# Gates made in the first stage, both orders summed token-major, strands by arrival

## The chip, the cores and the metric

The kernel runs on one core of a Trainium2 chip. Its engines have their own queues: TensorE (PE, matmuls; PEld is its weight load), VectorE (DVE), ScalarE (ACT), GpSimd (POOL), and SyncE (SP), which here issues all transfers. The metric is the device time of one execution, the median of several runs, in microseconds.

## The reference

Four layers follow each other on an image batch of 8 x 256 x 32 x 32: an attention with a gated feed-forward, a second attention with an MLP, a quantized bottleneck, and a selective scan (Mamba) over four orders of the pixels. The change lies in the last layer. Cut to what matters:

```python
xs = concat([rows, rows reversed, columns, columns reversed])   # each (b, L, 256), L = 1024
def _mamba(u, ...):
    x, z = split(u @ W_in.T, 2)                 # 512 channels each
    x = silu(causal_conv4(x) + conv_b)
    x_dbl = x @ W_x.T                           # dt (16), B (16), C (16)
    dt = softplus(x_dbl[:16] @ W_dt.T + b_dt)
    h = h * exp(dt * A) + dt * B * x            # 16 states per channel, in order of the tokens
    y = einsum(h, C) + x * D
    return (y * silu(z)) @ W_out.T
out = y1 + flip(y2) + transpose(y3) + transpose(flip(y4))
```

z depends on the pixel alone, so the four orders share one gate: the kernel sums y of the four orders first and multiplies the sum by silu(z) once.

## The kernel before

**Two stages.** `phase_a` does the first three layers for each sample, and then the sample's `mix`: the x half of the last layer's input projection, the causal convolution in both directions along rows (k = 0) and columns (k = 1), and silu, all stored to DRAM (`mixes`). The output of layer 2 is stored too, as bf16 `codes`. `phase_b` does the scans. It has 64 blocks: sample, then order (`swap` 0 rows, 1 columns), direction (`back`), and half of 512 tokens. A block has 16 steps, one for each state; a step has four scans (DVE), one for each 128 channels. So a sample has eight blocks.

**How the order of the work is made.** Each task is a generator, a strand. It yields an operation, a list of them, or a condition. `_Order.run` (L313) takes, among the strands whose next operation is ready, the one that could start first by a table of costs (L108 to L143), and among equal starts the one with the lowest `(rank, number)`, the number being the order in which strands were added. What it picks is emitted, so every engine's queue is in a fixed order before the kernel runs. `_Room`s are sets of buffers that strands take and put back. In both stages `keep_dense` (L276) adds filler matmuls on a constant tile (`minus`) where PE would stand idle for long.

**First stage.** `sample(b)` (L1141) has rank (2, b); its parts have ranks (0, b), (1, b), (3, b), `mix(b)` rank (2, b). So at equal starts an earlier sample goes first, its convolutions too. `mix` (L1164) runs for one sample at a time. For each of four channel chunks it projects 2 x 512 tokens (six bf16 matmuls each), copies the result from PSUM on DVE (L1205), makes four convolution branches of four DVE operations each over 1024 tokens, reorders rows to columns by a POOL copy (L1210), and ends each pair of branches with a batch of silu on ACT and a table load (L1184).

**Second stage.** For a step: ACT scales rows of dt\*x (`dbu`), PE transposes them to `db`; ACT makes `da` = exp(dt\*A); DVE scans; POOL multiplies the states by C (`h<-h,cb`); PE sums the products over the 16 steps into four banks `py`, token-major, by transposes that accumulate (`sums`, L1643). At the end of a block `moved` (L1676) takes py to the tile `yT`. The two directions of an order meet there: the second block of a forward pass and the first of a backward pass share py, the other two meet in yT by an addition. One PSUM bank, `pp`, is lent (L1338) to all side work: dt, the transposes of dt\*x, and what follows.

**Sums and gates before.** After the second and third block of every order, `fold` (L1459) transposes yT back to channels, four chunks for the half at hand, and copies it to the tiles `ys` (row order) or adds it to them through a transposed view (column order). `outputs(b, h)` (L1483) runs for half h of the sample before, in blocks 0 and 2 of the next sample: it loads the codes and z's weights, projects z (`project`, L1344), scales it on DVE, waits for a batch of silu that `tables` (L1436) joins with a softplus batch, multiplies ys by it on POOL (L1497), and makes two output products (`o3`, four matmuls of 512 columns each), which ACT copies and SP stores. For the last sample both halves come after the last scan.

Of the kernel before, what the change touches and what calls it, by code (L numbers as in the profile page):

```python
# [29 lines left out]
P = 128  # L30
# [46 lines left out]
def tile_conv_seq(ctx: ExitStack, tc: tile.TileContext, i: dict, out: bass.AP):  # L77
# [19 lines left out]
    ]  # L97

    parts = [dram.tile([P, CC, 3, P], BF16, name=f"w_in{m}", tag=f"w_in{m}") for m in range(2 * DC)]

    phase_a(tc, i, col, ident, codes, parts, mixes)
    phase_b(tc, i, col, ident, codes, parts, mixes, out)
# [242 lines left out]
def phase_a(ctx, tc, i, col, ident, codes, w_parts, mixes):  # L345
# [29 lines left out]
    RANK = lambda b: (2, b)  # L375
# [386 lines left out]
    def layer0(b, x):  # L762
        rank = b
# [103 lines left out]
    def feed_forward(b, x):  # L867


        rank = b  # L870
# [112 lines left out]
    def layer1(b, x):  # L983
        rank = b
# [179 lines left out]
    def mix(b):  # L1164


        def branch(c, k, src, back, left):
            o = yield from take(mx)

            def span(t, j):  # L1170
                return (t[:, : N - j], src[:, j:]) if back else (t[:, j:], src[:, : N - j])

            yield V.tensor_scalar(o, src, col("cv_w", 4 * c + PAD), col("cv_b", c), ALU.mult, ALU.add)
            for tap in range(PAD):
                to, x = span(o, PAD - tap)
                yield V.scalar_tensor_tensor(to, x, col("cv_w", 4 * c + tap), to, ALU.mult, ALU.add)
            left[back] = o

        def both(c, k, src):
            left = {}  # L1180
            for back in (False, True):
                order.add(RANK(b), branch(c, k, src, back, left))
            yield lambda: len(left) == 2
            ops = [A.activation(o, o, AF.Silu) for o in left.values()]  # L1184
            yield (2.58 + sum(o.cost for o in ops), ops + [_Table()])
            for back, o in left.items():
                yield S.dma_start(mixes[b][k][back][c], o)
                put(mx, o)

        def chunk(c):  # L1190
# [5 lines left out]
            for h in range(2):  # L1196
# [3 lines left out]
                yield [  # L1200
                    T.matmul(ps, lhsT=w[:, k, e], rhs=xc[:, k], start=(k == e == 0), stop=(k == CC - 1 and e == 2))
                    for k in range(CC) for e in range(3)
                ]
                put(low, xc)
                yield V.tensor_scalar(xi[:, hs(h)], ps, col("s3"), None, ALU.mult)  # L1205
# [4 lines left out]
            yield G.tensor_copy(xp.rearrange("p (b a) -> p b a", a=HH), xi.rearrange("p (a b) -> p b a", b=WW))  # L1210
# [32 lines left out]
    with tc.manual_schedule():  # L1243
        for b in range(B):
            order.add((2, b), sample(b))
        order.add((9, B), weight_parts())
        order.run()
# [14 lines left out]
def phase_b(ctx, tc, i, col, ident, codes, w_parts, mixes, out):  # L1262
# [23 lines left out]
    z_room = _Room(rooms, "z", DC, [P, HALF])  # L1286
    wi_room = _Room(rooms, "wi", 2, [P, CC, 3, P], BF16)
    xf_room = _Room(rooms, "xf", 1, [P, CC, HALF], BF16)
# [33 lines left out]
    yT = wp.tile([P, NT, DI], F32, name="yT", tag="yT")  # L1322
    ys = [wp.tile([P, N], F32, name=f"ys{c}", tag=f"ys{c}") for c in range(DC)]
# [5 lines left out]

    def load_x(b, h, box):  # L1330

        xf = yield from take(xf_room)
        yield S.dma_start(xf, codes[b][:, :, hs(h)].rearrange("k p n -> p k n"))
        box.append(xf)
# [8 lines left out]

    def project(box, m0):  # L1344


        yield lambda: bool(box)
        w = yield from take(wi_room)
        yield S.dma_start(w, w_parts[m0 // P])
        room, ps = yield from lend()  # L1350
        yield [
            T.matmul(ps, lhsT=w[:, k, e], rhs=box[0][:, k], start=(k == e == 0), stop=(k == CC - 1 and e == 2))
            for k in range(CC) for e in range(3)
        ]
        put(wi_room, w)
        box.append(None)
        if len(box) == DC + 1:
            put(xf_room, box[0])
        return room, ps
# [74 lines left out]
    gates = {(b, h): {} for b in range(B) for h in range(2)}  # L1434

    def tables(m=None, z=None):  # L1436

        def ready():
            return (m is None or len(raw[m]) == DC) and (z is None or len(gates[z]) == DC)

        yield ready
        ops = []
        if z is not None:
            ops += [A.activation(t, t, AF.Silu) for t in gates[z].values()]
        if m is not None:
            ops += [A.activation(t, t, AF.Softplus) for t in raw[m].values()]
        loads = 1 + (z is not None) + (m is not None)
        yield (1.28 * loads + sum(o.cost for o in ops), ops + [_Table()])
        if m is not None:
            blocks[m][0].done[blocks[m][1]].add("soft")  # L1450
        if z is not None:
            gates[z]["done"] = True

    clear = {0: True, 1: True}
    folds = {b: [0, 0] for b in range(-1, B)}
    given = {b: 0 for b in range(-1, B)}
    given[-1] = 2 * CC

    def fold(b, swap, h):  # L1459

        left = [DC]

        def one(c):
            yield lambda: (folds[b][0] == 2 * DC if swap else given[b - 1] == 2 * CC)
            room, ps = yield from lend()
            yield [
                T.transpose(ps[:, t * P : (t + 1) * P], yT[:, h * TH + t, c * P : (c + 1) * P], ident)
                for t in range(TH)
            ]
            left[0] -= 1  # L1470
            if not left[0]:
                clear[h] = True
            if swap:
                y = ys[c].rearrange("p (a b) -> p b a", b=WW)[:, 16 * h : 16 * h + 16]
                yield V.tensor_tensor(y, ps.rearrange("p (a b) -> p a b", b=WW), y, ALU.add)
            else:
                yield V.tensor_copy(ys[c][:, hs(h)], ps)
            put(room, ps)
            folds[b][swap] += 1

        return [one(c) for c in range(DC)]

    def outputs(b, h):  # L1483
        box, done = [], set()

        def first():
            yield from load_x(b, h, box)

        def gate(c):
            t = yield from take(z_room)  # L1490
            room, ps = yield from project(box, DI + c * P)
            yield V.tensor_scalar(t, ps, col("s3"), None, ALU.mult)
            put(room, ps)
            gates[b, h][c] = t
            yield lambda: "done" in gates[b, h] and folds[b][1] == 2 * DC
            y = ys[c][:, hs(h)]
            yield G.tensor_tensor(y, y, t, ALU.mult)  # L1497
            done.add(c)
            put(z_room, t)

        def o3(cc):
            yield lambda: len(done) == DC
            o = yield from take(z_room)
            room, ps = yield from lend()
            for c in range(DC):
                yield T.matmul(
                    ps, lhsT=w_o3[:, c, cc * P : (cc + 1) * P], rhs=ys[c][:, hs(h)],
                    start=(c == 0), stop=(c == DC - 1),
                )
            yield A.copy(o, ps)  # L1510
# [3 lines left out]
            given[b] += 1  # L1514
# [161 lines left out]
    def moved(n, d, h, py):  # L1676

        if n % 4 != 3:
            yield lambda: clear[h]
            clear[h] = False  # L1680
        for t in range(TH):
            o = yT[:, h * TH + t, :]
            if n % 4 == 3:
# [5 lines left out]
            put(py_room, py[t])  # L1689
        if n == len(blocks) - 1:  # L1690
            spare.append(py_room)
        if n % 4 > 1:
# [158 lines left out]
```

## Time and profile before

| what | us |
|---|---|
| median of 3 runs (9354.29 to 9357.71) | 9355.51 |
| the profiled execution's own time | 9359.27 |
| its span in the profile | 9357.5 |
| first scan | 3807.0 |
| end of the last scan | 9324.4 |

Busy time of the engines by stage, from windows of the trace:

| stage | length | PE | DVE | ACT | POOL |
|---|---|---|---|---|---|
| first | 3807.0 | 3540 | 3006 | 2676 | 370 |
| second | 5517.4 | 5154 | 5221 | 5314 | 5292 |
| tail | 33.1 | 27 | 9 | 6 | 13 |

PE's busy time holds the fillers (1994 of them in the first stage). Busy time in a row of the profile is the union over the row's instructions, and the mean is that of one from start to end; where instructions overlap, busy divided by count is shorter than the mean. Nearly all operations are issued from one line of a helper (L154), so groups are told apart by the names of their tiles.

### The profile page before, as it was taken

What the parts mean: (1) busy time and instruction counts of PE and PEld (TensorE: products, weight loads), DVE (VectorE), ACT (ScalarE), POOL (GpSimd) and SP (SyncE); (2) the same over time, 40 slices, a digit from 0 to 9 for tenths busy, and PEclk for the clock granted to TensorE, in tenths of its full rate; (3) what the DMA queues carried; (4) which work ended last, traced back from release to release, by engine and by line L of the source; (5) the groups of instructions that cost most, each with busy time, mean ns of one, the idle gap of its engine ahead of it and who ended that gap; (6) DMA issues with size and microseconds to landing.
All of it is one profiled execution on the core that took longest, in us unless ns stands there. A gap on an engine that the chain in (4) does not pass through costs nothing.

```text
span 9357.5 us, 152821 instructions
## 1 busy us (share of the span) xinstructions
PE 8721.1 (93%) x56752; PEld 5778.5 (62%) x56752; DVE 8236.6 (88%) x9134; ACT 7996.2 (85%) x15039; POOL 5674.9 (61%) x2742
## 2 busy tenths in 40 slices
PE   9999999999999998799999999999999999999998
PEld 3333333333333333688788788778788788787787
DVE  7688587969899777899999999999999999999898
ACT  7768576767777774899999999999999999999998
POOL 0010010101111100799999999999999999999999
PEclk9999999999999999999999999999999999999999
DMA  1100111111111112222222212212222222222221
GB/s 57 38 25 22 38 55 49 48 35 49 34 64 57 39 52 85 76 64 66 69 65 66 73 61 65 73 61 67 71 62 68 69 67 65 68 67 64 69 66 58
DMA packets 297420, 548.41 MB, mean 59 GB/s; under 512 B 31761, under 2 KB 98705, under 8 KB 291554
## 3 DMA queue, kind: packets, MB, share of 16 engines
q1 hardware_dynamic: 296674, 538.64, 17.8%
q8 instruction: 446, 7.31, 0.3%
q14 instruction: 300, 2.46, 0.1%
HBM read 427.90 MB, written 100.14 MB: 56 GB/s over the span
## 4 chain that ended last, share of the span: by engine, by line
ACT 24%; PE 24%; DVE 16%; issue 3%; POOL 1%; DMA 0%; DVEq 0%; SPq 0%; POOLq 0%; ACTq 0%
ACT da L154 11%; DVE h L154 11%; ACT dbu L154 9%; PE db L154 8%; PE py L154 7%; PE pp L154 5%; PE bank L154 3%; DVE mx L154 1%; DVE mid L154 1%; DVE stats L154 1%; DVE ys L154 1%; ACT dt L154 1%; ACT L154 1%; DVE yT L154 1%; ACT st L154 1%
## 5 line engine op out<-in xcount | busy, mean ns | idle before, releaser
L154 POOL TENSOR_TENSOR h<-h,cb 128x1024 f32<-128x1024 f32 x2048 | 4798.5, 2388 | 144.2 <-ACT st L154 79.8
L154 ACT ACTIVATE da<-dt,am 128x512 f32<-128x512 f32 x4096 | 2867.8, 714 | 138.5 <-DVE h L154 130.7
L154 DVE TENSOR_TENSOR_SCAN h<-da,db 128x512 f32<-128x512 f32 x2048 | 2330.3, 1199 | 227.9 <-PE db L154 132.2
L154 DVE TENSOR_TENSOR_SCAN h<-da,st,db 128x512 f32<-128x512 f32 x2048 | 2444.0, 1258 | 68.1 <-PE db L154 47.3
L154 ACT ACTIVATE dbu<-du,bT 128x512 f32<-128x512 f32 x3584 | 2476.9, 708 | 9.3 <-PE db L154 5.0
L154 PE MATMUL db<-ident,dbu 128*128 128x128 f32 x14336 | 2134.6, 277 | 316.0 <-DVE h L154 303.6
L154 PE MATMUL py<-ident,h 128*128 128x128 f32 x16384 | 2121.5, 273 | 10.4 <-POOL h L154 6.5
L154 PEld LDWEIGHTS db<-ident,dbu 128*128 128x128 f32 x14336 | 1614.4, 141 | 748.0 <-DVE h L154 486.2
L154 PEld LDWEIGHTS py<-ident,h 128*128 128x128 f32 x16384 | 1849.9, 140 | 29.9 <-POOL h L154 10.6
L154 ACT ACTIVATE bank<-bank,stats 128x512 f32<-128x512 f32 x1536 | 1018.8, 676 | 369.8 <-DVE stats L154 362.8
L154 DVE TENSOR_REDUCE stats<-bank 128x1 f32<-128x512 f32 x1536 | 976.4, 680 | 222.0 <-PE bank L154 218.0
L154 ACT ACTIVATE exps<-bank 128x512 f32<-128x512 f32 x1536 | 793.8, 612 | 194.7 <-PE bank L154 189.6
L154 PE MATMUL bank<-big,big 32*128 32x512 f32 x4096 | 873.8, 659 | 40.7 <-ACT bank L154 18.2
L154 DVE SCALAR_TENSOR_TENSOR mid<-mid,cols,mid 128x961 f32<-128x961 f32 (+2 forms) x560 | 726.0, 1296 | 12.5
L154 POOL COPY mx<-mx 128x1024 f32<-128x1024 f32 x28 | 64.4, 2301 | 903.6 <-DMA mix<-mx 534.9
L154 PEld LDWEIGHTS bank<-big,big 32*128 32x128 f32 x4096 | 297.5, 190 | 480.0 <-issue 209.9
L302 PE MATMUL bank<-minus 128*128 128x512 bf16 x1994 | 522.5, 404 | 37.7 <-ACT exps L154 17.5
L154 PE MATMUL db<-dg,du 128*128 128x128 f32 x4096 | 530.4, 279 | 17.0 <-DVE h L154 16.1
L154 PE MATMUL bank<-exps,big 128*32 128x512 f32 (+1 forms) x3072 | 538.7, 611 | 0.0
L154 POOL TENSOR_TENSOR mid<-mid,mid 128x512 f32<-128x512 f32 x64 | 102.6, 1623 | 689.8 <-DVE mid L154 630.4
L154 PEld LDWEIGHTS db<-dg,du 128*128 128x128 f32 x4096 | 488.7, 192 | 49.3 <-DVE h L154 26.3
L302 PEld LDWEIGHTS <-minus 128*128 128x128 bf16 x2080 | 197.4, 102 | 491.9 <-issue 294.3
(204 smaller groups left out, 9271.5 us busy)
## 6 DMA issues: line engine op xcount, KB each, us to landing
cb<-c_d SPq DMA_DIRECT2D x1024, 256.0 KB, 3.2
xs<-mix SPq DMA_DIRECT2D x256, 256.0 KB, 4.3
mix<-mx SPq DMA_DIRECT2D x112, 512.0 KB, 3.0
big<-in_x_dram SPq DMA_DIRECT2D x16, 1024.0 KB, 5.3
kept<-big SPq DMA_DIRECT2D x16, 1024.0 KB, 5.2
big<-kept SPq DMA_DIRECT2D x16, 1024.0 KB, 6.9
low<-codes SPq DMA_DIRECT2D x64, 256.0 KB, 3.7
wi<-w_in SPq DMA_DIRECT2D x64, 192.0 KB, 3.4
```

Of the source, the lines that this page charges most:

```text
L154: return getattr(getattr(nc, self.engine), self.method)(*self.args, **self.kw)
L302: self.nc.tensor.matmul(x, lhsT=self.minus, rhs=rhs, start=True, stop=True)
```

## The change

The gates move: `mix` projects z for 512 tokens beside each pair of branches, applies silu straight from PSUM in the same batch as the branches' silu, and stores it to a new DRAM tensor `gates`. `phase_b` only loads it, into ten buffers instead of four. In `mix` the copy of xi from PSUM and the reordering copy go from DVE and POOL to ACT.

The sums change: `yT` becomes two tiles, one for each order, and `fold` and `ys` go. For each chunk and half, `gate` gathers both orders in one bank: four transposes of the row order's tile, and on top eight matmuls with the column order's tile as weights and 64 columns of the identity as moving data, taken through a permuted view, written to four of every 32 positions. DVE multiplies the bank by the loaded gate. A gate waits until all sums of the sample are in (`full`). `outputs` runs in blocks 0 and 1 of the next sample instead of 0 and 2.

All ranks of the first stage lose the sample's number: equal starts go to the strand that was added first. The samples' own strands are added at the beginning, `mix` later.

```diff
-    RANK = lambda b: (2, b)
+    RANK = lambda b: (2, 0)
...
     def layer0(b, x):
-        rank = b
+        rank = 0
...
         def both(c, k, src):
             left = {}
...
+            yield lambda: left and DC + c in made
+            w, xc = yield from projected(DC + c, k)
             yield lambda: len(left) == 2
+            ps = yield from side()
+            yield project(ps, w, xc)
+            put(low, xc)
+            put(low, w)
+            z = yield from take(low)
             ops = [A.activation(o, o, AF.Silu) for o in left.values()]
+            ops.append(A.activation(z, ps, AF.Silu, scale=col("s3")))
             yield (2.58 + sum(o.cost for o in ops), ops + [_Table()])
-            for back, o in left.items():
-                yield S.dma_start(mixes[b][k][back][c], o)
+            back(ps)
+            yield S.dma_start(gates[b][c, :, hs(k)], z)
+            put(low, z)
+            for way, o in left.items():
+                yield S.dma_start(mixes[b][k][way][c], o)
                 put(mx, o)
...
-                yield V.tensor_scalar(xi[:, hs(h)], ps, col("s3"), None, ALU.mult)
+                yield A.activation(xi[:, hs(h)], ps, AF.Identity, scale=col("s3"))
...
-            yield G.tensor_copy(xp.rearrange("p (b a) -> p b a", a=HH), xi.rearrange("p (a b) -> p b a", b=WW))
+            yield A.copy(xp.rearrange("p (b a) -> p b a", a=HH), xi.rearrange("p (a b) -> p b a", b=WW))
...
         for b in range(B):
-            order.add((2, b), sample(b))
+            order.add((2, 0), sample(b))
...
-    z_room = _Room(rooms, "z", DC, [P, HALF])
-    wi_room = _Room(rooms, "wi", 2, [P, CC, 3, P], BF16)
-    xf_room = _Room(rooms, "xf", 1, [P, CC, HALF], BF16)
+    z_room = _Room(rooms, "z", 10, [P, HALF])
...
-    yT = wp.tile([P, NT, DI], F32, name="yT", tag="yT")
-    ys = [wp.tile([P, N], F32, name=f"ys{c}", tag=f"ys{c}") for c in range(DC)]
+    yT = [wp.tile([P, NT, DI], F32, name=f"yT{k}", tag=f"yT{k}") for k in range(2)]
...
-    def fold(b, swap, h):
...
+    turned = ident.rearrange("p (b a) -> p a b", b=4)
...
         def gate(c):
-            t = yield from take(z_room)
-            room, ps = yield from project(box, DI + c * P)
-            yield V.tensor_scalar(t, ps, col("s3"), None, ALU.mult)
-            put(room, ps)
-            gates[b, h][c] = t
-            yield lambda: "done" in gates[b, h] and folds[b][1] == 2 * DC
-            y = ys[c][:, hs(h)]
-            yield G.tensor_tensor(y, y, t, ALU.mult)
-            done.add(c)
-            put(z_room, t)
+            yield lambda: c in zz and full[b] == FULL
+            room, ps = yield from lend()
+            yield [
+                T.matmul(
+                    ps[:, t * P : (t + 1) * P], lhsT=yT[0][:, h * TH + t, c * P : (c + 1) * P], rhs=ident,
+                    is_transpose=True, start=(t == 0), stop=False, skip_group_check=True,
+                )
+                for t in range(TH)
+            ] + [
+                T.matmul(
+                    ps.rearrange("p (a b) -> p a b", b=WW)[:, :, 4 * t : 4 * t + 4],
+                    lhsT=yT[1][:, t, c * P : (c + 1) * P], rhs=turned[:, 16 * h : 16 * h + 16],
+                    start=False, stop=(t == NT - 1), skip_group_check=True,
+                )
+                for t in range(NT)
+            ]
...
+            yield V.tensor_tensor(zz[c], ps, zz[c], ALU.mult)
             put(room, ps)
+            left[1] -= 1
...
-            z = (d.b - 1, n % 8 // 2) if n > 4 and n % 8 in (0, 2) else None
+            z = (d.b - 1, n % 8) if n > 4 and n % 8 in (0, 1) else None
...
-                jobs.append((SOFT, tables(m, z)))
+                jobs.append((SOFT, tables(m)))
             if z is not None:
-                jobs += zip((0, 1, 3, 4, 5, 12, 13), outputs(*z))
+                jobs += zip((0, 1, 3, 5, 7, 9, 11), outputs(*z))
```

## The prediction

> **What bounds the kernel now.** I read the whole page first (busy shares and the forty slices), then windows cut at stage borders, then windows of one sample of the second stage block by block, then the rows of the operations that the change touches.
>
> The page's first two parts:
>
> ```profile
> span 9357.5 us, 152821 instructions
> PE 8721.1 (93%) x56752; PEld 5778.5 (62%) x56752; DVE 8236.6 (88%) x9134; ACT 7996.2 (85%) x15039; POOL 5674.9 (61%) x2742
> DVE  7688587969899777899999999999999999999898
> POOL 0010010101111100799999999999999999999999
> ```
>
> There are two regimes. Until the sixteenth slice GpSimd is idle; then four engines are full at once. The first scan starts at 3807 us and the last ends at 9324, so the first stage is 3807 us, the second 5517, the tail 33. The profiled execution took 9359.27 us, 1.8 over its span; the median of the runs is 9355.51, so 3.8 come off a sum made against the profile.
>
> The first stage in windows between the moments at which sample 2, 5 and 7 finish layer 2 (the stores of their codes), and to the stage's end; columns are PE, PE weight loads, DVE, ACT and POOL busy, then granted clock and DMA:
>
> ```profile
> 2051.00:3225.00 1174.00, 1103.35 (x5206) 416.64 (x5205) 1065.40 (x1414) 863.36 (x1840) 138.85 (x82) 0.95 0.14 49
> 3225.00:3674.00 449.00, 420.08 (x2150) 149.21 (x2147) 319.45 (x466) 303.75 (x598) 34.93 (x24) 0.95 0.17 62
> 3674.00:3774.00 100.00, 54.59 (x238) 23.68 (x236) 85.61 (x73) 35.79 (x31) 9.50 (x4) 0.80 0.30 111
> ```
>
> In the middle DVE is 91% busy: it is the bound there. Later it is 71%, and chains set the pace. The last 100 us are the convolutions of sample 7 alone, on DVE.
>
> The second stage, sample 3, cut at every 64th scan (one block of sixteen steps):
>
> ```profile
> 5862.00:5959.00 97.00, 90.35 (x661) 73.94 (x660) 85.11 (x85) 87.36 (x164) 85.79 (x42) 0.98 0.22 67
> 5959.20:6043.60 84.40, 78.60 (x623) 68.27 (x622) 81.35 (x76) 81.16 (x131) 82.94 (x40) 1.00 0.22 67
> 6043.60:6133.50 89.90, 86.30 (x644) 71.62 (x643) 79.50 (x79) 87.51 (x166) 84.66 (x42) 1.00 0.24 74
> 6133.50:6219.70 86.20, 81.12 (x650) 71.21 (x649) 84.38 (x81) 82.56 (x133) 84.39 (x40) 1.00 0.21 64
> 6219.70:6303.40 83.70, 77.92 (x616) 67.41 (x615) 81.00 (x82) 80.85 (x155) 76.63 (x37) 1.00 0.19 60
> 6303.40:6386.10 82.70, 76.36 (x611) 66.89 (x610) 80.72 (x75) 81.92 (x133) 82.70 (x39) 1.00 0.22 67
> 6386.10:6467.20 81.10, 76.40 (x610) 66.83 (x608) 76.28 (x74) 80.95 (x157) 81.10 (x39) 1.00 0.21 66
> 6467.20:6555.00 87.80, 81.27 (x641) 70.22 (x641) 86.04 (x81) 83.94 (x135) 85.27 (x41) 1.00 0.22 68
> ```
>
> Blocks 5 and 6 hold nothing but scans and their preparation: POOL is busy for all of 82.7 and 81.1 us. That is the floor. Blocks 0 and 2 carry a half of the gates and outputs of the sample before (+14.3 and +8.8 over it), blocks 0, 3, 4, 7 a fold (four groups of transposes, four additions or copies). The eight take 692.8 us where eight at the floor take some 655.
>
> The rows that price the change:
>
> ```profile
> L154 PE MATMUL pp<-ident,yT 128*128 128x128 f32 x496 | 85.5, 284 | 15.3 <-DVE ys L154 10.5 <-DVE yT L154 4.6
> L154 PE MATMUL py<-dd,xs 128*128 128x128 f32 x2048 | 268.9, 275 | 0.0
> L154 PEld LDWEIGHTS db<-dg,du 128*128 128x128 f32 x4096 | 488.7, 192 | 49.3 <-DVE h L154 26.3
> L154 PE MATMUL bank<-low,low 128*128 128x512 bf16 x384 | 98.1, 396 | 14.1 <-DMA low<-codes 12.0 <-DVE mx L154 1.0 <-ACT bank L154 0.6
> L154 ACT ACTIVATE big<-bank,temp 128x512 f32<-128x512 f32 x32 | 22.1, 694 | 36.9 <-PE bank L154 36.9
> L154 DVE TENSOR_SCALAR mx<-bank,cols 128x512 f32<-128x512 f32 x56 | 41.7, 745 | 67.3 <-PE bank L154 67.0
> ```
>
> Busy divided by count is the spacing: 0.131 us for a pass of an fp32 matmul over 128 columns (each such matmul is two passes: 2048 records for 1024 matmuls), 0.119 for its weight load.
>
> **Second stage, blocks without outputs.** All folds go, and the outputs move from blocks 0 and 2 to blocks 0 and 1 (the instruction order of the changed kernel has the gates at steps 2 to 7 and the two output products at steps 9 to 11 of both). What stays is the same block without its extras. Block 2 falls from 89.9 to the 81.6 that it took in the first sample, where it has no outputs (-8.3); block 3 from 86.2 to 82.7, like block 5 (-3.5); block 4 from 83.7 to 82.5 (-1.2); block 7 from 87.8 to 82.7 (-5.1). Sum -18.1 a sample. POOL holds them there: 32 products at 2.34 us (4798.5/2048), 5.1 for four tmp, 2.1 for two dg, 82.1 in all.
>
> **Blocks 0 and 1.** Four gate items now cost no ACT (four silu, one table load: 2.2 + 1.3), no POOL (5.0 of ys times z) and one DVE multiplication each of about 0.68 (the yT addition's row, same operands) in place of 0.74 and of the folds' 1.15. What is left is PE: four transposes at 0.156 (2.5/16 in block 3) and sixteen passes over 64 columns with a full weight load. No row has that shape. From above 0.131, the 128-column pass; from below 0.065, half of it (512 columns take 0.513, so columns count). I take 0.119, since the weight load isn't shortened. A gate is 0.62 + 1.90 = 2.53 us, four are 10.1, the output products 7.2 (their row in block 0). On a base of 76.4 (blocks 5, 6) that is 93.7 us of PE in a block, above POOL's 82: **PE becomes the bound of these two blocks.** With 3 us of gaps each (block 2 has 3.6) they need 193.4. But PE can put off the py transposes: in block 0 today they start up to 17 us after their product, elsewhere 4 to 5, and nine h buffers allow it. I give back 10: 183.4 against 181.4 now, +2. Ends: all hidden, 2 x 82.7, -16; or 0.131, nothing put off, gaps of 6.65 as in block 0, 202.3, +21. The waits "DVE h <- ACT da" 3.8 and "DVE h <- PE db" 5.0 in block 0 and their like in block 2 go with the silu batch, which held ACT for 8.9 us at a stretch; 5.1 remain (softplus).
>
> The Trainium skill, TensorE: Matmul & The Clock Gate, sections "Back-to-back issue gap" and "LDWEIGHTS (loading the stationary operand)", speaks against the halved columns: spacing comes from weight load and matmul together, and the load goes by its 128 columns, P/1.2. As an estimate 107 ns a pass; the two blocks would be 181.9 and the forecast some 12 us lower.
>
> Seven samples carry outputs: 7 x (-18.1 + 2) = -113, ends -239 and +20. The first sample gains in blocks 3, 4, 7 (85.1, 84.3, 87.8 to 82.7, 82.5, 82.7): -9. **Second stage -122 (-248 to +11).** The new wait, a gate for the last yT sum, has the next db transposes behind it on PE and the scans behind those; today's yT transposes wait for the same additions (4.6 us in their row, over the whole run).
>
> **Tail.** Now 26.0 us from the first yT transpose (9331.5) to the end: 8.4 until the output products, 13.9 of these, 3.7 for copy and store. The gates of both halves wait for the last sum, so PE runs 8 x 2.53 = 20.2 first, then the same. **+12** (0.065 to 0.131: +5 to +13).
>
> **First stage.** Added on ACT: 64 evictions of xi and 64 silu from PSUM at 0.69, 32 copies at 1.05 (the row of that size): 122 us. Off DVE: 56 x 0.745 + 8 x 0.744 = 48. Off POOL 74. PE gains 384 bf16 matmuls at 0.256 = 98 and has 387 filler matmuls of 0.262 fewer (101). SP issues 192 more transfers here and 16 fewer loads later (0.3 to 0.5 us each on a queue with 2000 in 9 ms). Behind the gate's store on SP stand the two stores of mix, which wait for the same silu batch anyway; behind the gates' loads in the second stage stand the cb loads, and the gates' ten buffers are free when they issue, so I price SP at nothing; a cb late by its 3.2 us of landing would show as POOL idle. The gate's projection takes two low buffers and one bank for some 6 us, so maxima, limited to three banks beside an attention, may wait; that is in the ends below.
>
> Ranks are equal now, so ties fall to the strand added first, and the convolutions of an early sample no longer go ahead of a later sample's layers. Pricing every DVE instruction of both orders by the mean of its row shows it: between the codes of samples 2 and 5 the work falls from 1070 us to 949, between 5 and 7 it grows from 319 to 371, after 7 from 82 to 120. ACT, priced alike: 840 to 805, then 298 to 369. Before sample 2 DVE is even, ACT +33.
>
> - Up to sample 2: no engine is bound (DVE 75%). 0 (-20 to +35, all added ACT on the path).
> - 2 to 5: at 91% DVE, 949 us are 1046, -128; some stalls aren't DVE's, so -100 (-128 to 0).
> - 5 to 7: chains; put-off work falls into DVE's 130 idle us. +15 (0 to +71).
> - After 7: 120 at the 86% of now is 140, +40 (+20 to +60).
>
> **First stage -45 (-128 to +166).** What hides the added ACT work is its 30% of idle time; if that cover goes, up to 122 show.
>
> **Sum.** 9357.5 - 45 - 122 + 12 = 9202.5, as a median about 9200.
>
> **Rivals.**
> 1. *ACT is the first stage's chain* (ends slower). For it: the last long chain of the page has 24% ACT, and "ACT bank <- DVE stats" makes both one chain. Against: ACT is 74% busy in the middle, DVE 91%. Price: all 122, nothing from DVE, and the late convolutions +40: +162, giving 9405. It decides once the first stage loses over 129.
> 2. *PE eats the second stage's gain*: the upper end above, +11 and +13: 9357.5 - 45 + 24, as a median 9333. For it: PE is 93% busy in block 0. Against: py has been put off before.
> 3. *All at POOL's floor*: -248 and +9: 9070. For it: POOL is full in blocks 5 and 6 with PE at 92%. Against: 17 us more of PE per block.
>
> **How the numbers follow.** Forecast 0.65, rivals 0.11, 0.13, 0.11. No change means within 0.2% (19 us), about what a measurement here can tell. Rival 2 lies at that border: half of it is the same. Slower is rival 1 and a little of both stages failing. Faster 0.81, same 0.06, slower 0.13. The likeliest alone is 9110 to 9290; to hold 8 in 10 the range goes to rivals 3 and 2: 9070 to 9340.
>
> **What would show it.** Second stage: blocks 2, 3, 4, 7 at 81 to 83 us with POOL full; blocks 0 and 1 at 88 to 95 with PE over 95% busy; spacing of the 64-column passes 0.10 to 0.13; no POOL rows of ys. First stage: its end near 3760, sample 5's codes some 100 us earlier, the DVE-only end near 140 us. It is wrong if blocks 0 and 1 pass 100 us, or if sample 5's codes come no earlier than 3225.

## The result and the profile after

The changed kernel takes 9284.88 us (median of four runs, 9275.05 to 9289.06), against 9356.61 of the kernel before on the same chip: a ratio of 0.9915 with a 95% interval of 0.9903 to 0.9927, so 68 to 91 us less, where some 155 were forecast. The profiled execution has a span of 9287.3 us. Its first scan starts at 3807.2 (3807.0 before), its last scan ends at 9239.3, and the tail is 48.1. So **all of the gain lies in the second stage (-85), the tail gives 15 back, and the first stage gains nothing.**

From the first two parts of its page:

```profile
span 9287.3 us, 153572 instructions
PE 8701.5 (94%) x57003; PEld 5821.0 (63%) x57097; DVE 8034.5 (87%) x8940; ACT 8059.9 (87%) x15119; POOL 5517.7 (59%) x2648
DVE  7688677787987976899999999999999999899998
POOL 0010010000001000699999999999899899899998
```

DVE has 202 us less to do and POOL 157 less, ACT 64 more. GpSimd has no row of `ys` left.

The first stage in windows between the stores of the codes of samples 2, 5 and 7, and to its last convolution; columns are PE, PE weight loads, DVE, ACT and POOL busy, then granted clock, DMA and GB/s:

```profile
2021.00:3123.00 1102.00, 1044.91 (x4870) 388.64 (x4903) 924.33 (x1268) 831.40 (x1742) 93.04 (x62) 0.95 0.18 61
3123.00:3645.00 522.00, 485.72 (x2420) 177.31 (x2441) 365.85 (x526) 377.96 (x729) 31.81 (x24) 0.95 0.21 72
3645.00:3774.00 129.00, 90.38 (x373) 37.99 (x377) 117.25 (x103) 87.24 (x83) 0.00 (x0) 0.92 0.60 204
```

Sample 2's codes are 30 us earlier than before, the stretch to sample 5 is 72 shorter, that to sample 7 is 73 longer, and the end 29 longer: it sums to nothing. In the long stretch DVE is only 70% busy and ACT 72%.

Sample 3 of the second stage, cut at every 64th scan, with the same columns:

```profile
5836.70:5928.40 91.70, 90.27 (x713) 79.68 (x712) 82.07 (x82) 84.19 (x161) 82.48 (x39) 1.00 0.25 73
5928.40:6022.30 93.90, 91.40 (x719) 80.10 (x717) 83.71 (x79) 83.42 (x134) 82.94 (x39) 1.00 0.23 67
6022.30:6103.10 80.80, 75.38 (x597) 65.41 (x596) 76.89 (x75) 80.61 (x157) 75.96 (x37) 1.00 0.21 61
6103.10:6186.90 83.80, 77.28 (x615) 67.17 (x613) 80.69 (x75) 82.24 (x132) 83.80 (x40) 1.00 0.22 67
6186.90:6269.80 82.90, 77.94 (x613) 67.15 (x612) 79.37 (x79) 81.33 (x158) 79.43 (x38) 1.00 0.21 62
6269.80:6353.60 83.80, 77.30 (x614) 67.17 (x613) 80.69 (x75) 82.25 (x132) 83.80 (x40) 1.00 0.24 67
6353.60:6435.80 82.20, 76.83 (x616) 67.46 (x615) 76.79 (x75) 81.94 (x159) 82.17 (x39) 1.00 0.23 65
6435.80:6519.10 83.30, 77.24 (x617) 67.59 (x616) 81.32 (x76) 82.00 (x133) 83.30 (x40) 1.00 0.26 77
```

A sample takes 682.4 us instead of 692.9. Blocks 0 and 1 have PE busy for all but 1.4 and 2.5 us. In blocks 3, 5, 6 and 7 POOL is full.

Rows of block 0 (busy time and mean ns of one, then idle before):

```profile
L155 PE MATMUL pp<-ident,yT 128*128 128x64 f32 x64 | 8.0, 293 | 0.0
L155 PE MATMUL pp<-z,w_o 128*128 128x512 f32 x16 | 7.2, 592 | 0.0
L155 DVE TENSOR_TENSOR z<-pp,z 128x512 f32<-128x512 f32 x4 | 2.8, 691 | 3.7 <-PE pp L155 3.7
```

64 passes over 64 columns take 8.0 us. Divided by the count that is 0.125 us, but this figure is not the spacing: the passes overlap, and the last of each burst stays in the sum with its whole 0.293 us, which weighs less the longer the burst is. The timeline of block 0 gives the spacing from start to start:

```profile
5857.38 2.44 PE L155 MATMUL pp<-ident,yT 128*128 128x128 f32 x20
5859.65 0.62 PE L155 MATMUL db<-ident,dbu 128*128 128x128 f32 x4
5860.10 1.06 PE L155 MATMUL py<-dd,xs 128*128 128x128 f32 x8
5860.99 0.60 PE L155 MATMUL db<-ident,dbu 128*128 128x128 f32 x4
```

A gate's 20 passes (4 transposes over 128 columns, 16 passes over 64) take 2.27 us, 0.114 a pass; eight passes over 128 columns, whose row in the prediction divides into 0.131, take 0.89, 0.111 a pass. **A pass over 64 columns is no shorter than one over 128.**

### The profile page after: what moved, and what is told of

Read it like the earlier page. It is cut to its first block, busy times and chain, and to the rows that moved or that the text cites. A ratio compares the mean times of both kernels' runs of the same rounds, so it can differ in the third digit from the quotient of the medians.

```text
span 9287.3 us, 153572 instructions
## 1 busy us (share of the span) xinstructions
PE 8701.5 (94%) x57003; PEld 5821.0 (63%) x57097; DVE 8034.5 (87%) x8940; ACT 8059.9 (87%) x15119; POOL 5517.7 (59%) x2648
## 4 chain that ended last, share of the span: by engine, by line
PE 29%; ACT 19%; DVE 17%; issue 4%; POOL 1%; DMA 1%; SPq 0%; POOLq 0%; DVEq 0%; ACTq 0%
DVE h L155 11%; PE db L155 10%; ACT da L155 9%; PE py L155 8%; ACT dbu L155 7%; PE pp L155 6%; PE bank L155 4%; DVE mid L155 1%; DVE mx L155 1%; DVE stats L155 1%; POOL h L155 1%; ACT dt L155 1%; ACT st L155 0%; ACT L164 0%; ACT L155 0%
## 5 line engine op out<-in xcount | busy, mean ns | idle before, releaser
L155 PE MATMUL db<-ident,dbu 128*128 128x128 f32 x14336 | 2112.4, 277 | 285.5 <-DVE h L155 268.9
L155 PE MATMUL bank<-big,big 32*128 32x512 f32 x4096 | 884.8, 666 | 18.2 <-ACT bank L155 9.0
L155 POOL TENSOR_SCALAR big<-big,ga,gs 128x512 f32<-128x512 f32 x64 | 75.1, 1186 | 1081.4 <-DVE gs L155 752.6
L155 DVE SCALAR_TENSOR_TENSOR mid<-mid,cols,mid 128x961 f32<-128x961 f32 (+2 forms) x560 | 705.6, 1260 | 11.5
L303 PE MATMUL bank<-minus 128*128 128x512 bf16 x1607 | 428.4, 402 | 42.0 <-ACT exps L155 16.6
L155 PE MATMUL bank<-big,wr 128*128 128x512 f32 x896 | 448.2, 630 | 17.8 <-ACT bank L155 8.5
```

The source lines that it names most:

```text
L155: return getattr(getattr(nc, self.engine), self.method)(*self.args, **self.kw)
L303: self.nc.tensor.matmul(x, lhsT=self.minus, rhs=rhs, start=True, stop=True)
```

## The experiments

Three questions were open: why the first stage gained nothing, what sets the length of blocks 0 and 1, and whether SP's queue has a price. "First scan" below is the length of the first stage in the profile.

### First stage: which part does what

The two halves of the change, each alone. `arrival_alone` is the kernel before with equal ranks (the middle edit stands in three places):

```diff
-    RANK = lambda b: (2, b)
+    RANK = lambda b: (2, 0)
...
-        rank = b
+        rank = 0
...
-            order.add((2, b), sample(b))
+            order.add((2, 0), sample(b))
```

> The kernel before with the equal ranks alone; gates and second stage as before. Theory P (the equal ranks only put DVE work off: the middle of the first stage gains some 100 us, the end gives it back, and the added ACT work is hidden): first scan 3777 to 3837 us, whole time 9325 to 9385. Theory Q (the equal ranks gain, and the gain is lost because xi and its reordered copy now come from ACT, so that the convolution's first DVE operation waits in ACT's queue): first scan near 3735, whole time near 9285.

9356.37 us, ratio 0.9998 (0.9988 to 1.0007); first scan 3803.6, and a second stage as before. Sample 5's codes come at 3064 instead of 3225, sample 7's at 3646 instead of 3674.

`ranks_by_sample` is the changed kernel with the same lines turned back.

> The changed kernel with the ranks of before; gates, copies on ACT and second stage as changed. Theory P: first scan 3790 to 3830, whole time 9265 to 9310. Theory Q: the middle isn't relieved and the waits on ACT stay, so the first scan comes at 3850 or later and the whole time is 9325 or more.

9354.42 us, ratio 0.9992 (0.9983 to 1.0002); first scan 3874.9, the second stage as in the changed kernel.

`copies_back` is the changed kernel with the eviction of xi on DVE and the reordering copy on POOL again:

```diff
-                yield A.activation(xi[:, hs(h)], ps, AF.Identity, scale=col("s3"))
+                yield V.tensor_scalar(xi[:, hs(h)], ps, col("s3"), None, ALU.mult)
...
-            yield A.copy(xp.rearrange("p (b a) -> p b a", a=HH), xi.rearrange("p (a b) -> p b a", b=WW))
+            yield G.tensor_copy(xp.rearrange("p (b a) -> p b a", a=HH), xi.rearrange("p (a b) -> p b a", b=WW))
```

> The changed kernel with the xi eviction back on DVE and the reordering copy back on POOL. Theory Q: the late waits of DVE on ACT (73.8 us between the codes of samples 5 and 7) go, first scan 3735 to 3770, whole time 9215 to 9250. Theory P: DVE has 48 us more and the first scan comes at 3807 to 3850, whole time 9285 to 9325.

9341.09 us, ratio 0.9978 (0.9968 to 0.9988); first scan 3862.7.

Set side by side: ranks alone gain 3 us (3807.0 to 3803.6), which is nothing that can be read. Gates and copies under the old ranks cost 68 (to 3874.9). Under equal ranks the gates alone cost 59 (3803.6 to 3862.7) and the move of the two copies to ACT gives 55 back (to 3807.2). **So equal ranks do not speed up the stage alone; together with the copies' move they hide the gates.** ACT, which the forecast had as a cost with a cover, was the better place under equal ranks: moved to it, 96 copies shortened the stage. The 73.8 us for which DVE waits for ACT's reordering copies in the changed kernel were no price either: without them the stage is longer. What in the gates costs the 59, their work on PE and ACT, their bank or their buffers, was not taken apart. Of the expectations, `arrival_alone` came as theory P had it, `ranks_by_sample` as theory Q, and `copies_back` as neither.

The first scan has a spread of its own: seven kernels whose first stage is the same instruction for instruction (the changed kernel and six variants of its second stage below) gave 3792.4 to 3812.8. Differences under some 20 us are not read here.

### First stage: why 102 us at sample 5's codes are gone by sample 7's

Suspect one: the convolutions put off to the end. `late_mix_first` gives those of the last three samples precedence:

```diff
-    RANK = lambda b: (2, 0)
+    RANK = lambda b: (2, -1 if b >= 5 else 0)
```

> The changed kernel with the convolutions of samples 5, 6 and 7 ahead of the other strands of their rank, so that they fill DVE between the codes of samples 5 and 7 instead of waiting for the end. Theory P: the codes of sample 5 stay near 3123, the DVE-only end shrinks from 129 us to about 100, first scan 3745 to 3785. Theory Q: waits on ACT set the late pace whatever the ranks, first scan 3800 to 3820.

9309.07 us, ratio 0.9941 (0.9926 to 0.9956); first scan 3811.9. The end after sample 7's codes shrinks from 129 to 92 us, and those codes come 41 us later (3686): nothing gained. The first scan lies where the second expectation has it, but that expectation's reason, waits on ACT, fell with `copies_back`.

`light_mix` takes work away: for samples 5 and 6 the three multiply-adds of each convolution branch are left out (its first, a multiplication, stays), so its output is not the reference's.

```diff
-            for tap in range(PAD):
+            for tap in range(0 if b in (5, 6) else PAD):
```

> The changed kernel with three of four taps of the convolutions of samples 5 and 6 left out (their x is wrong), 123 us less DVE work in the late part of the first stage. Theory P (the DVE work put off is what the late part pays for): first scan 3690 to 3745. Theory T (sample 7's own chain of feed-forward, attention, layer 2 and convolutions sets the late pace, and other samples' DVE work runs beside it): the codes of sample 7 stay within 25 us of 3645, the DVE-only end shrinks by 20 to 40, first scan 3760 to 3790.

9274.51 us (one run); first scan 3792.4. Window between the codes of samples 5 and 7, columns as above:

```profile
3129.00:3666.00 537.00, 490.94 (x2509) 180.06 (x2510) 288.87 (x467) 409.11 (x760) 32.61 (x24) 0.97 0.26 90
```

DVE has 77 us less to do than in the changed kernel's 522 us (288.87 for 365.85), and the stretch is no shorter. So the put-off convolutions are not what lengthens it, and the theory that held them responsible fell. The end after sample 7's codes shrinks from 129 to 93 us; 21 of these 36 are lost again because the codes come later (3666), and the 15 that are left lie within the stage's own spread. The other theory on record, that sample 7's own chain sets the late pace, had the codes and the end about right; the next run tests it.

Suspect two: sample 7 itself comes late to its second attention, at 3297 instead of 3229. `feed7_first` lets its feed-forward go ahead:

```diff
-            order.add((3, rank), chunk(o))
+            order.add((1.5 if b == 7 else 3, rank), chunk(o))
```

> The changed kernel with the feed-forward chunks of sample 7 ahead of the main strands (rank 1.5 instead of 3). Theory T (sample 7's own chain sets the late pace): its second store of x, at the start of its second attention, comes 20 to 50 us before 3297 and the first scan at 3765 to 3795. If the attention of sample 6, which holds the banks until 3280, sets it instead, the store comes earlier but its end (the load at 3571) and the first scan don't move: 3795 to 3815.

9376.55 us, ratio 1.0016 (1.0007 to 1.0026); first scan 3900.3. Sample 7 enters at 3154, 143 us earlier, and its attention ends at 3588, 17 us later than in the changed kernel. The end grows from 129 to 207 us, with DVE 156 of it busy: 78 of the 93 us lost lie there, behind sample 7's codes. Neither outcome on record came (a first scan at 3765 to 3795, or at 3795 to 3815): an earlier entry alone is worth nothing.

What the traces show is an order between the attentions. The second attention of a sample has a pass of row maxima (tile `stats`) and then one of exponentials (`exps`). Windows of the instructions of `stats` in the changed kernel, DVE and ACT busy; the borders are the passes of samples 5 (end), 6 and 7:

```profile
2855.00:3005.00 150.00, 4.39 (x10) 3.02 (x9) 0.98 0.26 91
3005.00:3163.00 158.00, 78.19 (x125) 89.05 (x244) 0.92 0.14 46
3163.00:3321.00 158.00, 5.39 (x12) 5.37 (x15) 0.97 0.26 87
3321.00:3463.00 142.00, 81.35 (x136) 90.93 (x257) 0.94 0.10 35
3463.00:3575.00 112.00, 0.57 (x3) 0.28 (x1) 1.00 0.26 91
```

and in the kernel before:

```profile
2901.00:3048.00 147.00, 7.19 (x15) 7.17 (x20) 0.97 0.22 76
3048.00:3186.00 138.00, 76.07 (x124) 85.89 (x240) 0.88 0.10 36
3186.00:3322.00 136.00, 10.85 (x19) 8.62 (x25) 0.99 0.17 61
3322.00:3501.00 179.00, 76.12 (x124) 86.90 (x245) 0.91 0.11 39
3501.00:3565.00 64.00, 0.90 (x5) 0.54 (x3) 1.00 0.21 77
```

Maxima hardly run while another sample's exponentials do (4 to 11 us of DVE in 136 to 158): the code holds them to three banks beside an attention. So the passes of samples 6 and 7 form a single file, nearly all of them 110 to 180 us long, and by this reading the file, not an engine's amount of work, sets when sample 7's codes come. By the rows' start times, the exponentials of sample 5 end 48 us earlier than before (2991 for 3039), the maxima of sample 6 begin 43 earlier, the exponentials of sample 6 end 27 earlier (3299 for 3326), and the maxima of sample 7 begin at the same time (3321 for 3322), since now sample 7's own feed-forward ends only at 3297 and leaves a gap of 22 us in the file. **Of the 102 us at sample 5's codes only 48 were ever in this file;** the other 54 are sample 5's feed-forward, which no longer waits behind convolutions (132 us from its exponentials to its codes, 186 before). In `feed7_first` the maxima of sample 6 begin at 3088 instead of 3005, and those of sample 7, begun earlier (3283 for 3321), end later (3503 for 3458): what sample 7 gained, sample 6 ahead of it in the file lost. The single file is read from the traces; no run with more banks for the maxima was made, so that they are its only cause is not shown.

### Second stage: what sets blocks 0 and 1

PE is full there, so the plain theory is that its work sets them. `no_column_sums` leaves the column order's eight matmuls of each gate out (the outputs lack the column orders):

```diff
-                    is_transpose=True, start=(t == 0), stop=False, skip_group_check=True,
+                    is_transpose=True, start=(t == 0), stop=(t == TH - 1), skip_group_check=True,
...
-                for t in range(NT)
+                for t in range(0)
```

> The changed kernel without the eight 64-column matmuls of each gate, so the output lacks the column order's two directions. Theory R (PE is the bound of blocks 0 and 1): 64 passes at 0.124 us go from each, 7.9 us, and the blocks fall from 91.7 and 93.9 to between 83 and 86.5; a sample from 682.4 to some 667; the end after the last scan from 48 to about 32 us; whole time 9155 to 9190. Theory S (the one lent bank or the gate's DVE multiplication sets them): they stay above 89 and the whole time above 9235.

9236.17 us (one run). Blocks 0 and 1 of sample 3:

```profile
5826.00:5916.00 90.00, 86.16 (x660) 73.29 (x659) 81.40 (x82) 83.80 (x159) 82.14 (x39) 1.00 0.24 76
5916.00:6006.00 90.00, 84.86 (x644) 71.51 (x643) 83.28 (x79) 83.33 (x135) 82.82 (x39) 1.00 0.21 69
```

8.0 us of passes fewer in each block shorten it by 1.7 and 3.8 us only, and PE now idles for 4 to 5. PE's amount of work is not what the blocks cost above POOL's 82, at least no longer once 8 us are gone. The 83 to 86.5 us that the theory of a PE bound asked for did not come. The blocks stayed above 89, as the other theory on record asked, but the traces speak against what it names. The one lent bank is held, from the first write of each loan to its last read, for 43 us of each of these blocks in the changed kernel and for 52 in `apart` (below), where they are shorter. The gates' multiplications on DVE wait for `pp` for 3.7 and 3.2 us in the changed kernel and in no wait that the profile lists here, and the blocks still take 90. What stays is the scans' wait for `db`: 5.9 and 4.8 us in the changed kernel, 6.9 and 4.5 here.

`late_products` moves the two output products on by two blocks (steps 6 and 13 of blocks 2 and 3):

```diff
-                jobs += zip((0, 1, 3, 5, 7, 9, 11), outputs(*z))
+                made = outputs(*z)
+                jobs += zip((0, 1, 3, 5, 7), made[:-CC])
+                waiting[n + 2] = made[-CC:]
+            jobs += zip((6, 13), waiting.pop(n, ()))
```

> The changed kernel with the two output products of each half two blocks later, steps 6 and 13 of blocks 2 and 3, where PE has some 6 us to spare a block. Theory R: blocks 0 and 1 lose 6 to 7 us each, blocks 2 and 3 gain 1 to 4 each, a sample takes 670 to 677, whole time 9225 to 9260. Rival (PE's 94% over the whole sample is the bound, not its share in two blocks): blocks 2 and 3 grow by what 0 and 1 lose, 9275 to 9295.

9286.65 us, ratio 0.992 (0.9905 to 0.9935). Blocks 0 and 1 fall by 3.1 and 3.3 us, blocks 2 and 3 rise by 2.4 and 4.2: a product costs about the same wherever it stands. That is what the rival on record expected, which holds PE's sum over a whole sample to be the bound; but in `no_column_sums` PE has some 16 us less to do in a sample, and the sample is 5.5 shorter (676.9).

`outputs_0_2` puts the outputs back into blocks 0 and 2, as in the kernel before:

```diff
-            z = (d.b - 1, n % 8) if n > 4 and n % 8 in (0, 1) else None
+            z = (d.b - 1, n % 8 // 2) if n > 4 and n % 8 in (0, 2) else None
```

> The changed kernel with the second half's gates and output products in block 2 instead of block 1, as before the change. Theory R: block 1 falls to 83 to 85, block 2 rises to 90 to 93, the sum of the three within 4 us of 266.4, whole time 9260 to 9310. If PE's put-off work carries from block 0 into block 1 (block 1 is 2.2 us dearer than block 0 with the same outputs), a sample gains 4 to 8 us: 9230 to 9260.

9255.17 us, ratio 0.9888 (0.9872 to 0.9905). The first three blocks of sample 3:

```profile
5823.20:5915.40 92.20, 90.79 (x716) 80.15 (x715) 82.59 (x83) 84.69 (x162) 83.15 (x39) 1.00 0.21 70
5915.40:5998.10 82.70, 77.31 (x615) 67.35 (x614) 80.73 (x75) 81.38 (x132) 81.01 (x39) 1.00 0.23 74
5998.10:6087.30 89.20, 88.46 (x708) 78.96 (x707) 79.53 (x78) 83.72 (x159) 82.08 (x39) 1.00 0.23 70
```

264.1 us for 266.4, between the two expectations. A sample takes 678.5, the second stage 5404.6 instead of 5432.0.

`apart` breaks the bursts: a gate is issued in three parts of four matmuls, the product's matmuls one at a time, with at least one scan between parts:

```diff
+    scanned = [0]
+
+    def apart(b):
+        k = scanned[0]
+        yield lambda: b == B - 1 or scanned[0] > k
...
-            yield [
+            parts = [
...
+            for t in range(0, len(parts), 4):
+                yield from apart(b)
+                yield parts[t : t + 4]
...
+                yield from apart(b)
...
+                scanned[0] += 1
```

> The changed kernel with each gate's twelve matmuls issued in three parts of four, and each output product's four matmuls one by one, with at least one scan's issue between them; the same work in the same blocks. Theory U (what blocks 0 and 1 pay for is the burst: 2.5 to 3.6 us of PE at a stretch outlast the three db banks, and the scans that wait are not caught up): blocks 0 and 1 fall from 91.7 and 93.9 to between 85 and 89, a sample from 682.4 to some 672, whole time 9215 to 9250. Theory R (PE's total in these blocks): they stay above 90.5, whole time 9270 to 9295.

9252.63 us, ratio 0.9888 (0.9874 to 0.9903). Blocks 0 and 1 take 90.9 and 91.2 us (91.7 and 93.9 in the changed kernel), a sample 678.8 (means of the samples with outputs), the second stage 5406.2. The blocks stay above 90.5, as theory R had it, and the whole time lies between the ranges of both theories. So bursts are a part of the cost, 3.5 us of some 20, and the 85 to 89 us expected if they were all of it did not come.

`apart_0_2` has both edits.

> The same spacing, with the second half's gates and products in block 2 instead of 1. Theory U: blocks 0 and 2 at 84 to 88, a sample 666 to 674, whole time 9190 to 9235. Theory R: like outputs in blocks 0 and 2 without spacing, a sample 678, whole time 9245 to 9265.

9258.32 us, ratio 0.9892 (0.9877 to 0.9907). Blocks 0, 1, 2 take 90.8, 83.8 and 89.6 us, a sample 678.2: the two gains do not add.

By their medians `apart` and `outputs_0_2` beat both kernels: 26 to 27 us of their 30 to 32 lie in the second stage, the rest is within what the first stage varies.

What holds blocks 0 and 1 at 90 with 8 us less of gates on PE is open. In the changed kernel the two take some 20 us more than two blocks at POOL's pace (185.6 less 2 x 82.7), and no single edit, to PE's work, to the bursts or to the place of the products, took more than 6.4 of that off.

### SP's queue

`late_loads` asks for the loads of xs at step 4 of a block instead of step 1:

```diff
-                jobs += zip((1, XD), mixed(k))
+                jobs += zip((4, XD), mixed(k))
```

> The changed kernel with one number changed: the four loads of xs for the block after next are issued at step 4 of a block instead of step 1. At step 1 the fourth of them finds its buffer still held by the block at hand, SP waits some 5 us for it, and the next load of C (cb) stands behind it. In the changed kernel GpSimd waits 48.6 us in 28 places of the second stage for nothing that the profile shows, most of it 1.8 to 2.6 us in block 0 at 28 us from its start, which is where that cb would be late. Theory SP (the prediction priced SP at nothing; that was wrong, and the queue behind the xs loads is part of what blocks 0 and 1 cost): those waits fall from 48.6 to under 10 us, blocks 0 and 1 take 2 to 5 us less together (185.6 to 181-183.5), a sample 678 to 680.5 instead of 682.4, the second stage 5403 to 5420 instead of 5432, the whole 9256 to 9273. Theory Q (the wait is real but hidden: GpSimd has slack in blocks 0 and 1, since PE and DVE set their pace): the waits go or move, blocks 0 and 1 stay within 1 us of 185.6, the sample within 1 us of 682.4, and the whole stays at 9285 within what the first stage varies (about 16 us).

9281.06 us, ratio 0.9915 (0.9901 to 0.9928). Waits of POOL, us in total, times and longest, in the second stage of the changed kernel

```profile
POOL h L155 <- ACT st L155: 95.9, 46, 7.9
POOL h L155 <- issue: 48.6, 28, 2.6
```

and of this one

```profile
POOL h L155 <- ACT st L155: 95.7, 46, 7.9
POOL h L155 <- issue: 47.7, 28, 2.4
```

Nothing moved: blocks 0 and 1 stay at 91.6 and 93.9. But the edit was too weak to decide. The loads had waited for their buffers until then in any case; only in block 2 did a load of C go ahead of them, and that block stayed at 80.8. Neither theory is told apart by it. The unexplained waits fell to 10.5 us in `apart` and 14.8 in `outputs_0_2`, with their xs loads placed in the same way, which speaks against the queue as their cause, though not strongly, and shows no other.

## Why the prediction was right, and where its steps failed

The sign, the range and the place of most of the gain (the second stage) held; the size did not, 9285 for 9200: 70 of the 155 us came. The range held 9285 because it allowed for a first stage that gains nothing and blocks 0 and 1 that cost more. By its steps:

- **First stage, -45: failed; it was 0.** *Up to sample 2 and 2 to 5* (0 and -100) measured -30 and -72, together -102. That the sum agrees is in part luck: 30 of it came where nothing was forecast, and in the stretch from 2 to 5 DVE, taken as its bound, was busy for 924 us, 84% and no longer 91%. *5 to 7* (+15, end +71) measured +73: this is the term that was mis-sized, by 58 us. It was worked out as DVE work falling into DVE's idle time. The idle time was there and the work fit; what was missing, by the traces, was the single file of attention passes, in which the forecast's milestone, the codes of sample 5, is not a member. That it is the only cause is not shown. *After 7* (+40) measured +29.
- **What hides the added ACT work:** named as ACT's 30% of idle time. Against that, under the old ranks gates and copies cost 68 us, and of the edits that moved work onto ACT the copies saved 55 under equal ranks. The added work was hidden in the end; that ACT's idle time is what hid it is not shown.
- **Second stage, -122: right in kind, -85 in size.** Per sample it forecast -16.1 and got -10.5. Blocks 2 and 3 together came within 0.3 us (164.6 for 164.3); blocks 4 and 5 took 1.4 more and 6 and 7 took 1.7 more than forecast, and blocks 0 and 1 took 185.6 for 183.4. These 5.6 us, in six samples, are 34 of the 37 us missing. The floor per block was taken from blocks 5 and 6 of the kernel before, each by itself. POOL's work is 81.7 us a block on average (653.9 for the eight windows), but POOL still waits in blocks 2 and 4 for `st`, the copies of the scans' last states on ACT:

```profile
POOL h L155 <- ACT st L155: 3.7, 1, 3.7
POOL h L155 <- issue: 1.1, 1, 1.1
```

  (block 2; block 4 has 3.3 of the first kind, where the kernel before had 3.0.) Block 4 itself came within 0.4 us; the excess lies in blocks 5, 6 and 7, where POOL is full, and why they take 2.8 more than forecast is open. The last sample gained 18 us where 16 were forecast, the first 6 for 9.
- **Blocks 0 and 1:** "PE becomes the bound" was right as a reading (98 and 97% busy) and its number within 2.2 us, but the runs do not confirm its reason: with 8 us of passes fewer in each the two blocks fall by 5.5 us together, not by 16. The number is near in part because its terms offset each other: PE was busy for 181.7 us in the two where 187.4 less 10 put off had been worked out, and idle for 3.9 where 6 had. The py transposes started up to 16 us after their product in block 0 and up to 8 in block 1; the kernel before had 17 and 10 there, and 16 and 13 in blocks 2 and 7, not 4 to 5. So the room for putting work off was in use before the change.
- **The pass over 64 columns:** taken at 0.119 between 0.065 and 0.131. The step that failed is "busy divided by count is the spacing": by that reading a pass over 64 columns takes 0.124 to 0.125, from start to start it takes 0.114, and one over 128 columns 0.111 and not 0.131. So the columns, which the prediction let count for a tenth, do not count at all here; whether the strided writes of these passes have a part in it was not tested. The Trainium skill's TensorE: Matmul & The Clock Gate, section "LDWEIGHTS (loading the stationary operand)", makes the load P/1.2, an estimate of 107 ns a pass for 128 columns. The measured 111 and 114 ns lie 4 and 7 above it: for the 64 columns it is no nearer than the 119 taken, but that halving them saves nothing agrees with it.
- **Tail, +12:** +15, for another reason in part. The timeline of PE in the tail:

```profile
9251.53 13.85 PE L155 MATMUL py<-ident,yT 128*128 128x128 f32 x120
9265.20 7.04 PE L155 MATMUL py<-z,w_o 128*128 128x512 f32 x16
9272.08 4.66 PE L155 MATMUL py<-ident,yT 128*128 128x128 f32 x40
9276.57 7.05 PE L155 MATMUL py<-z,w_o 128*128 128x512 f32 x16
```

  From the first transpose to the end it is 35.8 us for 26.0 before, +9.8 where +12 was forecast: the eight gates take 18.2 us (13.67 and 4.49, from start to start) for the 20.2 worked out from the wrong spacing. From the last scan to that transpose it is 12.2 us for 7.1, +5 where nothing was forecast: POOL still has four products to finish, before it had two. The rows of the tail after and before:

```profile
L155 POOL TENSOR_TENSOR h<-h,cb 128x1024 f32<-128x1024 f32 x4 | 9.4, 2466 | 0.0
L154 POOL TENSOR_TENSOR h<-h,cb 128x1024 f32<-128x1024 f32 x2 | 4.7, 2401 | 0.0
```

- **SP at nothing:** waits of POOL that the profile leaves unexplained appear in blocks 0 and 1 (5.7 us in the two). That a load of C behind the xs loads makes them was looked for and not found; open.
- **Rivals:** the first (ACT is the first stage's chain) fell: the stage lost nothing, and under equal ranks the copies' move onto ACT shortened it. The second (PE eats the gain) came true in part: blocks 0 and 1 rose by 4.2 us where +2 was forecast and +21 was its end. The third fell with blocks 0 and 1 at 92 and 94.

## What to carry to other kernels

A milestone that moves tells the end of a stage only if it lies on the chain that ends it: follow the exclusive resource (here a right to banks that lets one attention pass run at a time), and ask what each pass waits for, before summing an engine's work between milestones. That an engine is 98% busy in a block does not tell what relieving it is worth; take work from it and see how far the block follows. Where instructions overlap, busy time divided by their number is not their spacing: read the spacing from starts in the timeline. Parts of a change that gain nothing alone can still be needed together: in this order ranks gained 3 us, gates cost 59 and the copies' move gained 55; all of them together came out at nothing, for a second stage that is 85 us shorter.

## What the runs showed of the hardware

- Halving the moving columns of an fp32 matmul from 128 to 64 did not shorten the spacing of its passes: 0.114 us from start to start with 64 (gates, a fifth of whose passes are transposes), 0.111 with 128; with 512 columns and weights of the same size it is 0.43 (16 passes in 6.88 us, 9265.20 to 9272.08).
- Busy time divided by count gave 0.125, 0.131 and 0.45 for the same passes: a short burst looks slower by it.
- The same first stage, in the same order on every engine, began its first scan anywhere from 3792.4 to 3812.8 us in seven profiles, 0.5%, while the changed kernel's samples 1 to 6 (counted from 0) repeated within 0.5 us (682.4 to 682.8).
- Eight us less work on the busiest engine shortened two blocks by 1.7 and 3.8 us, and output products moved on by two blocks cost there (6.6) what they had saved (6.4).
